# Soft MoE on one Trainium2 core: dispatch weights turned by VectorE, expert products in column halves, loads by use

## The chip, the cores and the metric

The kernel runs on one core of one Trainium2 chip. The metric is the device time of one execution in microseconds (us): 777.72 us in the median of three runs (777.15 to 778.01). About 0.2% is what such runs can tell from no change.

## What is computed

The input x has 8 sequences of 256 tokens and 128 channels. Six sublayers follow each other, each on the layer norm of x: a soft mixture of experts (half weight), linear attention, the same mixture again (half weight), a gated network of five 128/512 layers (half weight), an attention with random features, and the gated network again (half weight). The change is in the mixture. For each sequence:

```python
x = layernorm(x, norm_g, norm_b)                      # (n, d): 256 tokens, 128 channels
se = layernorm(slot_embeds, slot_g, slot_b) * scale   # (e, s, d): 16 experts, 64 slots each
logits = einsum('bnd,esd->bnes', x, se)
dispatch = softmax(logits, axis=1)                    # over the tokens
combine = softmax(logits.reshape(b, n, -1), axis=-1)  # over the 1024 slots
slots = einsum('bnd,bnes->besd', x, dispatch)
gate = gelu(einsum('besd,edf->besf', slots, Wg) + bg)
up = einsum('besd,edf->besf', slots, Wu) + bu         # f: 256
eout = einsum('besf,efo->beso', gate * up, Wd) + bd
out = einsum('bns,bso->bno', combine, eout)
```

All is in fp32.

## The kernel before, in words

**Order of the work.** The kernel is written as steps. A step (class `Step`) names the engines that can do it with a planned cost in ns, what it reads and writes, and the buffers it takes. `Plan.place` (line 122) is a list scheduler: it gives each step an engine, a start and a buffer slot, by earliest start and then by a key. `LAG` (line 73) is the planned delay from one engine's end to another's start. The key follows the PE work planned so far, plus a shift for each part of the program (`SHIFTS`, line 16), numbers that a search has found. `issue` (line 193) emits all instructions in order of planned start; each engine then runs its own list strictly in that order on the chip, and waits on semaphores. DMAs are mostly issued from SP's queue.

**Groups.** The 8 sequences form two groups of four (`group`, line 1286). Group 1's keys are set 45,000 ns behind those of group 0, so that the two groups interleave. Within a group: dispatch of four sequences, 16 experts on the slots of all four, combine and linear attention per sequence; the second mixture; the gated network; the random features; the gated network again, which stores the result.

**Keys** (line 448). The slot embeddings are normalized, turned by TensorE (`flip`, line 355: a transpose against the identity, line 356) and stored as `seT`, with a third copy (line 489) so that odd sequences can read the two halves of a 128-slot block in reversed order.

**Dispatch** (line 523), once per sequence and mixture, 16 times in all. `norm` and `normalized` (line 373) make y: statistics on VectorE, the root on GpSimd (lines 392 and 393), the application on GpSimd or VectorE (line 399). `transposed` (line 419) turns y; `logits` (line 537) has four rounds of two matmuls, copied to `comb` by `evacuated` (line 358; ScalarE line 363 or VectorE line 365), and a running maximum (line 554). Then, for each half of 512 slots: the maximum over tokens (569), exponentials with sums (577), reciprocal (585), division on GpSimd (590). The result `ex` has slots on partitions; the gather needs tokens there. So TensorE turns it in 128-squares (`turn`, line 598: eight flips per half, copied from PSUM to `dm` in two copies of 128x512) and `gathered` (611) makes two fp32 matmuls of 512 columns. `affinely` (436) puts the result, with gain and bias of the norm, into `sl`. At last the maximum over slots is turned (639), reduced, spread over the partitions (651, matmuls against the identity), subtracted on GpSimd (663) and exponentiated (669), for the combine.

**Experts** (line 675). `fetch` (684) loads an expert's matrices and its bias `bd`. `front` (694) makes gate and up (703), GELU (709) and the product (714). `back` (726) makes, for each expert, four matmuls with 128 stationary columns, which are 64 slots of two sequences, and 128 moving columns (733), and adds the bias in two operations of 64 partitions (743). The outputs overwrite the slots of the block in `sl`.

**Buffers** (line 229): `comb` 9 of 8 KB per partition, `k4` 6, `we` 3, eight PSUM banks, and others.

**Loads.** All weights of the other sublayers are loaded at the start (`load`, line 260), the small vectors one by one, from the queues of SP, ScalarE and GpSimd. x is loaded in pairs of sequences (282 and 289), the embeddings in halves from ScalarE's queue (279).

The attention with random features already uses tiles of TensorE's array: `projected` (line 1168) runs four 32-row tiles, `products` (line 1261) four 32-column tiles.

Of the kernel before, what the change touches and what calls it, by code (L numbers as in the profile page):

```python
# [16 lines left out]
    -1227, -613, -401, -68, -58, -18, -64, -450, -1382, -1020, -424, -281, -256, -288, -233,  # L17
    -157, -79, -415, -2474, -2414, -2140, -1616, -1392, -1410, -1361, -1647, -1993, -981, -1024,
    -765, -300, -356, -285, -548, -633, -125, 202, -436, 1069, 1221, 47, 271, -1474, 20, 20,
    328, 135, 321, 41, 324, 244, 344, -354, 285, -285, 130, -858, -387, -2, -20, -1081, -1196,  # L20
    -1025, -690, 2, -62, -155, -432, -31, 11, 73, 364, -325, 423, 704, 1277, 1488, 0, -230,
    -498, -161, 261, 336, -1069, -2039, -294, 15, -985, -97, 217, 334, -2546, -904, 699, 282,
    280, 343, -499, -1613, -348, 575, -245, 854, 1080, -1505, 7, 181, -43, 85, 275, 63, 263,
    275, -549, 207, -31, 105, -21, -515, -1151, -524, -514, -318, -600, -516, -298, -150, -63,
    -195, -1899, -1808, -1825, -1479, -1755, -1468, -2181, -1630, -332, -1392, -135, -1924,
    -2484, -1986, -1337, -312, -863, 129, -9, -422, 292, 66, 420, 268, 35, 18, 226, 263, 558,
    1104, 691, -956, -1572, -901, -704, -964, -1303, -1243, -1820, -2476, -2535, -1146, -830,
    -744, 683, -666, -1356, -722, 275, 396, -1669, -293, -1310, -784, 170, 576, 457, 239, 57,
    785, 684, 309, 781, 1213, 1341, 704, 927, 758, 229, 1188, -1400, 467, 1275, -975, 2, 61,
    -923, 156,  # L30
# [34 lines left out]
class Plan:  # L65
# [7 lines left out]
    LAG = {"PE": 300, "ACT": 120, "DVE": 100, "POOL": 150, "SP": 2200}  # L73
# [128 lines left out]
def macaron_kernel(ctx: ExitStack, tc: tile.TileContext, i: dict, out: bass.AP):  # L202
# [27 lines left out]
        "comb": (NJ * N, 9),  # L230
        "slots": (NJ * NB * 4 * S1, G),
        "k4": (1024, 6),
# [3 lines left out]
        "we": (6 * P + D, 3),  # L236
# [5 lines left out]


    for at, cells in (
        (5000, ["begin"]), (7000, [("x", b) for b in range(B)]), (7500, ["small"]),
        (15000, ["weights"]),
    ):
        plan.given(at, cells)
# [11 lines left out]
    def load(name, shape, src=None, eng=nc.sync):  # L260
        t = const.tile(shape, F32, tag=name, name=name)
        eng.dma_start(t, i[name] if src is None else src)
        return t


    x = const.tile([P, NT, D], F32, tag="x", name="x")
    xin = i["L0_attn_x"].rearrange("b (p t) d -> p b t d", t=TT)
    xout = out.rearrange("b (p t) d -> p b t d", t=TT)

    def x_of(b, n=1):  # L270
        return x[:, b * TT : (b + n) * TT, :].rearrange("p (b t) d -> p b t d", t=TT)

    se_raw = Buf("k4", (P, NJ, D))
    sein = i["slot_embeds"].rearrange("(j p) d -> p j d", p=P)
    for h in range(2):
        part = slice(4 * h, 4 * h + 4)
        step(
            {"SP": 100},
            lambda _, part=part: nc.scalar.dma_start(se_raw.ap[:, part], sein[:, part]),
            ["begin"], [(se_raw, h)],  # L280
        )
    nc.sync.dma_start(x_of(0, 2), xin[:, 0:2])
    sg = load("slot_g", [P, 1], eng=nc.scalar)
    sb = load("slot_b", [P, 1], eng=nc.scalar)
    sc = load("scale", [P, 1], i["scale"].partition_broadcast(P), eng=nc.scalar)
    ng = load("norm_g", [P, 1])
    nb = load("norm_b", [P, 1])
    for q in range(1, 4):
        nc.sync.dma_start(x_of(2 * q, 2), xin[:, 2 * q : 2 * q + 2])
# [60 lines left out]
    def flips(n):  # L350
        return 110 * n
# [164 lines left out]

# [858 lines left out]
```

## Time and profile before

| | us |
|---|---|
| median of three runs | 777.72 |
| the profiled execution | 777.5 |
| its span, first to last instruction | 775.8 |
| busy: PE (matmul) | 754.0 |
| busy: VectorE (DVE) | 528.2 |
| busy: ScalarE (ACT) | 450.4 |
| busy: GpSimd (POOL) | 351.2 |

The page gives for each engine the busy time and the count of instructions, and for groups of instructions their line, tiles, shape, count, busy time and mean duration. An fp32 matmul of the source appears as two instructions, a flip as one. Matmuls are pipelined, so their durations overlap; what one costs is the distance between starts. PEld is the load of stationary operands, beside PE. A window row gives the busy time of each engine in a stretch of the span.

### The profile page before, as it was taken

What the parts mean: (1) busy time and instruction counts of PE and PEld (TensorE: products, weight loads), DVE (VectorE), ACT (ScalarE), POOL (GpSimd) and SP (SyncE); (2) the same over time, 40 slices, a digit from 0 to 9 for tenths busy, and PEclk for the clock granted to TensorE, in tenths of its full rate; (3) what the DMA queues carried; (4) which work ended last, traced back from release to release, by engine and by line L of the source; (5) the groups of instructions that cost most, each with busy time, mean ns of one, the idle gap of its engine ahead of it and who ended that gap; (6) DMA issues with size and microseconds to landing.
All of it is one profiled execution on the core that took longest, in us unless ns stands there. A gap on an engine that the chain in (4) does not pass through costs nothing.

```text
span 775.8 us, 12408 instructions
## 1 busy us (share of the span) xinstructions
PE 754.0 (97%) x4584; PEld 631.6 (81%) x4584; DVE 528.2 (68%) x1156; ACT 450.4 (58%) x824; POOL 351.2 (45%) x376
## 2 busy tenths in 40 slices
PE   2999999999999999999999999999999999999998
PEld 1768787898888988888889879889777887868787
DVE  4899888668988788885645453566865458885422
ACT  1888999555977689987443332345544327543422
POOL 6969454524618356248932123533721326424210
PEclk9999999999999999999999999999999999999999
DMA  7102323203231123232432200000000000000000
GB/s 195 40 0 64 89 65 118 68 29 116 72 114 34 56 68 96 73 86 76 135 95 67 80 1 1 1 1 1 1 1 1 0 15 1 1 1 1 14 0 28
DMA packets 27579, 36.96 MB, mean 48 GB/s; under 512 B 3808, under 2 KB 18816, under 8 KB 27520
## 3 DMA queue, kind: packets, MB, share of 16 engines
q1 hardware_dynamic: 25968, 35.62, 15.6%
q8 instruction: 36, 0.59, 0.3%
q10 hardware_dynamic: 1488, 0.53, 0.3%
q14 instruction: 23, 0.19, 0.1%
q0 software_dynamic: 64, 0.03, 0.0%
HBM read 35.12 MB, written 1.05 MB: 47 GB/s over the span
## 4 chain that ended last, share of the span: by engine, by line
PE 95%; POOL 1%; DVE 1%; DMA 1%; ACT 0%; SPq 0%; issue 0%; POOLq 0%
PE ps L990 25%; PE ps L703 14%; PE ps L772 7%; PE ps L733 7%; PE ps L611 7%; PE ps L537 7%; PE ps L356 6%; PE ps L1090 4%; PE ps L1060 4%; PE ps L1063 4%; PE ps L1230 2%; PE ps L1168 1%; PE ps L1261 1%; PE ps L820 1%; PE ps L651 1%; PE ps L1154 1%
## 5 line engine op out<-in xcount | busy, mean ns | idle before, releaser
L363 ACT COPY k<-ps 128x512 f32<-128x512 f32 (+1 forms) x99 | 51.6, 533 | 128.2 <-PE ps L990 79.7
L703 PE MATMUL ps<-slots,we 128*128 128x256 f32 x512 | 121.0, 380 | 0.0
L703 PEld LDWEIGHTS ps<-slots,we 128*128 128x128 f32 x512 | 93.8, 189 | 16.6 <-issue 4.3
L990 PE MATMUL ps<-comb,comb 128*128 128x256 f32 x448 | 102.8, 380 | 0.0
L990 PE MATMUL ps<-comb,slots 128*128 128x256 f32 x448 | 101.9, 381 | 0.0
L663 POOL TENSOR_TENSOR comb<-comb,k 128x1024 f32<-128x1024 f32 x32 | 75.1, 2365 | 57.3 <-ACT k L577 29.6
L990 PEld LDWEIGHTS ps<-comb,slots 128*128 128x128 f32 x448 | 83.8, 190 | 13.4 <-issue 1.9
L990 PEld LDWEIGHTS ps<-comb,comb 128*128 128x128 f32 x448 | 83.4, 190 | 11.8 <-issue 1.4
L975 POOL TENSOR_TENSOR comb<-comb 128x512 f32<-128x512 f32 x20 | 30.6, 1530 | 123.9 <-ACT comb L1012 73.3
L590 POOL TENSOR_TENSOR k<-k,sm 128x1024 f32<-128x1024 f32 x32 | 60.6, 1903 | 35.7 <-DVE sm L585 34.3
L356 PE MATMUL ps<-ident,k 128*128 128x128 f32 x408 | 60.1, 276 | 15.1 <-POOL k L399 13.6
L714 DVE SCALAR_TENSOR_TENSOR k<-ps,bu,k 128x256 f32<-128x256 f32 x128 | 57.3, 477 | 22.7 <-ACT k L709 21.7
L709 ACT ACTIVATE k<-ps,bg 128x256 f32<-128x256 f32 x128 | 56.4, 473 | 26.1 <-PE ps L703 25.2
L1004 DVE TENSOR_TENSOR comb<-ps,k 128x512 f32<-128x512 f32 x48 | 33.0, 688 | 55.2 <-PE ps L990 31.9
L356 PEld LDWEIGHTS ps<-ident,k 128*128 128x128 f32 x408 | 49.0, 143 | 26.0 <-POOL k L399 14.6
L733 PEld LDWEIGHTS ps<-we,k 128*128 128x128 f32 x512 | 63.9, 192 | 4.9 <-issue 2.4
L743 DVE TENSOR_TENSOR slots<-ps,we 64x256 f32<-64x256 f32 x128 | 53.8, 421 | 20.3 <-PE ps L733 17.4
L537 PE MATMUL ps<-k,seT 128*128 128x256 f32 x256 | 63.4, 389 | 2.5 <-ACT k L441 1.6
L733 PE MATMUL ps<-we,k 128*128 128x128 f32 x512 | 65.4, 275 | 0.0
L577 ACT ACTIVATE k<-comb,sm 128x256 f32<-128x256 f32 x128 | 63.3, 497 | 1.4 <-DVE sm L569 1.2
L1012 ACT ACTIVATE comb<-comb 128x512 f32<-128x512 f32 x48 | 29.9, 628 | 54.2 <-DVE comb L1004 54.1
L772 PE MATMUL ps<-slots,comb 128*128 128x129 f32 x512 | 60.4, 275 | 0.0
(144 smaller groups left out, 1425.5 us busy)
## 6 DMA issues: line engine op xcount, KB each, us to landing
we<-in_We SPq DMA_DIRECT2D x64, 384.0 KB, 3.1
we<-in_bd SPq DMA_DIRECT2D x64, 64.0 KB, 3.1
x<-in_L_attn_x SPq DMA_DIRECT2D x4, 256.0 KB, 5.8
comb<-in_h2T SPq DMA_DIRECT2D x4, 256.0 KB, 3.3
slots<-in_h1T SPq DMA_DIRECT2D x4, 256.0 KB, 4.9
out<-x SPq DMA_DIRECT2D x8, 128.0 KB, 1.7
k<-in_slot_embeds ACTq DMA_DIRECT2D x2, 256.0 KB, 6.2
k<-in_hs SPq DMA_DIRECT2D x2, 256.0 KB, 4.3
```

The lines of the kernel that those rows point to most:

```text
L356: nc.tensor.transpose(po, src, ident)
L537: mm(pl.ap[:, j, :], seT[:, 2 * u + j, odd : odd + 2].rearrange("p k s -> p (k s)"), yt.ap, start=True, stop=True,)
L577: nc.scalar.activation(ex.ap[:, j, :], comb.ap[:, 4 * h + j, :], AF.Exp, bias=mx.ap[:, j : j + 1], accum_out=mx.ap[:, 4 + j : 5 + j],)
L590: nc.gpsimd.tensor_tensor(ex.ap, ex.ap, mx.ap[:, 8:12].unsqueeze(2).to_broadcast([P, 4, N]), ALU.mult)
L611: mm(po.ap.rearrange("p j k s -> p (j k s)"), y.ap[:, t, :], dm.ap[:, t, :], start=(t == 0), stop=(t == TT - 1),)
L663: nc.gpsimd.tensor_tensor(raw, raw, mb.ap.unsqueeze(1).to_broadcast([P, 4, N]), ALU.subtract)
L703: mm(pe.ap[:, m, :], we.ap[:, ts(2 * m + c, P)], sl.ap[:, j, :, k::2, 0:S], start=True, stop=True,)
L709: nc.scalar.activation(ga.ap, pe.ap[:, 0, :], AF.Gelu, bias=bg[:, e, c : c + 1])
L714: nc.vector.scalar_tensor_tensor(ht.ap[:, c, :], pe.ap[:, 1, :], bu[:, e, c : c + 1], ga.ap, ALU.add, ALU.mult,)
L733: mm(po.ap[:, q, :], ht.ap[:, c, ts(q, P)], we.ap[:, ts(4 + c, P)], start=(c == 0), stop=(c == 1),)
L772: mm(po.ap[:, t, 0 : D + 1], comb.ap[:, j, ts(t, P)], eo()[:, j, q, 0 : D + 1], start=(j == 0), stop=(j == NJ - 1),)
L990: mm(bank.ap[:, o], w(k)[:, c, ts(o, P)], rhs().rearrange("p (c n) -> p c n", c=2)[:, c, :], start=(start and o + c == 0), stop=(stop and ...
```

## The change

**Turned on VectorE.** `ex` is now one `comb` buffer for all 1024 slots. VectorE transposes each half in place, in squares of 32 (two instructions of 128x1024 per dispatch). The 16 flips, their four copies to `dm` and `dm` are gone. After such a turn, the partitions 32a to 32a+31 hold 32 tokens, for the slots 32a to 32a+31 of every block. So each of the four groups of 32 rows needs all tokens of y in its own 32 partitions: `replicated` writes y to DRAM (four DMAs) and reads it back four times (four DMAs) into `yr`, all from SP. `gathered` makes 8 x 4 matmuls with 32 rows, each row group into its own PSUM bank, and each bank is put into `sl` by `affinely`, 256 columns at a time.

**Down products.** `back` now handles a pair of experts: the two experts' slots go to the two halves of the partitions, by tiles of 64 columns, and one 128x512 operation adds both biases. `sl` and `seT` change their layout for it, and the third copy in `seT` goes. `back` of a pair follows the `front` of the expert after it.

**Loads.** x, embeddings and one packed `small` come first, from SP in steps that the plan orders: x one sequence at first, the keys in quarters. The other weights (`later`) may be loaded only behind the first copy of y. `keys` works in quarters.

**Other.** `spread` uses flips. The norm's root negates the mean (one GpSimd instruction more) so that the application adds; the addition of 1e-6 on GpSimd becomes a multiplication by 1 and an addition. At the start ScalarE runs one exponential on a constant and TensorE 14 matmuls of the identity by itself (`rehearse`). `comb` has 10 buffers, `k4` 4, `we` 4. SP's planned lag is 2600 ns instead of 2200, some planned costs change, and all shifts are new.

```diff
-            for t in range(TT):
-                pt = ps_(4, P)
...
-                step({"PE": flips(4)}, turn, [ex], [pt], takes=[dm])
-                evacuated(
...
+            def turn(_, part=part):
+                nc.vector.transpose(
+                    ex.ap[:, part].rearrange("p j n -> p (j n)"),
+                    ex.ap[:, part].rearrange("p j n -> p (j n)"),
+                )
+
+            step({"DVE": 1200}, turn, [(ex, h)], [(ex, h)])
+
+        pos = [ps_(NJ, 32) for _ in range(4)]
+
+        def gathered(_):
+            for c in range(N // 32):
+                for a, po in enumerate(pos):
+                    rows = slice(32 * a, 32 * a + 32)
                     mm(
-                        po.ap.rearrange("p j k s -> p (j k s)"), y.ap[:, t, :], dm.ap[:, t, :],
-                        start=(t == 0), stop=(t == TT - 1),
+                        po.ap, yr.ap[rows, c, :], ex.ap[rows, :, 32 * c : 32 * c + 32],
+                        start=(c == 0), stop=(c == N // 32 - 1), tile_position=(32 * a, 0),
                     )
+        step({"PE": 3600}, gathered, [yr, (ex, 0), (ex, 1)], pos)
+
+        for a, po in enumerate(pos):
             affinely(
-                lambda h=h: sl.ap[:, 4 * h : 4 * h + 4, q // 2, blocks, 0:S],
-                lambda po=po: po.ap, [po], [(sl, j, q) for j in range(4 * h, 4 * h + 4)], 512,
+                lambda a=a: sl.ap[:, :, a // 2, q, 32 * (a % 2) : 32 * (a % 2) + 32],
+                lambda po=po: po.ap, [po], [(sl, "in", q, a)], NJ * 32,
             )
```

```diff
+    def replicated(y, b):
+
+        yr = Buf("k4", (P, N // 32, D))
+
+        def spill(_):
+            for k in range(4):
+                nc.sync.dma_start(
+                    spilled[b].rearrange("i (t k) d -> i k t d", k=4)[:, k],
+                    y.ap[32 * k : 32 * k + 32],
+                )
+
+        def spread(_):
+            for a in range(4):
+                nc.sync.dma_start(yr.ap[32 * a : 32 * a + 32], spilled[b])
```

```diff
             def down(_):
-                for q in range(NB):
+                for q in range(BG):
                     for c in range(2):
-                        mm(
-                            po.ap[:, q, :], ht.ap[:, c, ts(q, P)], we.ap[:, ts(4 + c, P)],
-                            start=(c == 0), stop=(c == 1),
-                        )
+                        for k in range(2):
+                            mm(
+                                po.ap[S * k : S * k + S, q, :], hts[k].ap[:, c, ts(q, S)],
+                                wes[k].ap[:, ts(4 + c, P)], start=(c == 0), stop=(c == 1),
+                                tile_position=(0, S * k),
+                            )
...
             def biased(_):
-                for u in range(2):
-                    rows = slice(u * S, (u + 1) * S)
-                    nc.vector.tensor_tensor(
-                        eo()[rows, j, (u ^ k) :: 2, 0:D], po.ap[rows],
-                        we.ap[rows, 6 * P :].unsqueeze(1).to_broadcast([S, NB, D]), ALU.add,
-                    )
+                nc.vector.tensor_tensor(
+                    eo()[:, j, :, 0:D], po.ap,
+                    wes[0].ap[:, 6 * P :].unsqueeze(1).to_broadcast([P, BG, D]), ALU.add,
+                )
```

```diff
         def spread(_):
             for t in range(TT):
-                mm(
-                    pb.ap[:, ts(t, P)], mn.ap[:, t : t + 1].to_broadcast([P, P]), ident,
-                    start=True, stop=True,
-                )
+                flip(pb.ap[:, ts(t, P)], mn.ap[:, t : t + 1].to_broadcast([P, P]))
...
+    plan.key = -100000
+    x_in(0, 1)
+    keys_in(0)
+    fetched(lambda: small, i["small"], [], ["small", "ng"])
+    keys_in(1)
+    x_in(1, 1)
+    keys_in(2)
+    keys_in(3)
...
+    def rehearse(_):
+        for _ in range(14):
+            mm(pwarm.ap, ident, ident, start=True, stop=True)
```

## The prediction

> **What bounds the kernel now.** I read the page first, for the engine shares and the chain that ended last.
>
> ```profile
> PE 754.0 (97%) x4584; PEld 631.6 (81%) x4584; DVE 528.2 (68%) x1156; ACT 450.4 (58%) x824; POOL 351.2 (45%) x376
> ...
> PE 95%; POOL 1%; DVE 1%; DMA 1%; ACT 0%; SPq 0%; issue 0%; POOLq 0%
> ```
>
> TensorE (PE) is busy nearly throughout and 95% of the chain is its own work. Second, the windows by stage (columns: stretch, its length, busy time of PE, PEld, DVE, ACT, POOL, clock, DMA share, GB/s):
>
> ```profile
> 0.00:11.30 11.30, 0.00 (x0) 0.00 (x0) 3.10 (x18) 1.28 (x1) 4.89 (x22) 1.00 0.68 203
> 11.30:22.45 11.15, 6.76 (x21) 4.32 (x21) 7.64 (x34) 3.65 (x6) 10.45 (x17) 1.00 0.71 200
> 22.45:57.70 35.25, 34.66 (x173) 26.13 (x174) 32.05 (x56) 31.07 (x90) 27.49 (x23) 1.00 0.00 1
> 57.70:140.00 82.30, 80.94 (x445) 66.11 (x444) 69.73 (x144) 77.53 (x146) 49.74 (x37) 1.00 0.29 85
> 140.00:500.00 360.00, 359.54 (x2215) 312.39 (x2215) 246.10 (x588) 218.21 (x413) 166.42 (x191) 1.00 0.23 67
> ```
>
> See two regimes. After 140 us PE alone is full. From 22 to 140 us VectorE (DVE) and ScalarE (ACT) are at 85 to 94% beside it: there they are nearly as late as PE. Before 22 us PE waits for data.
>
> A busy PE says little of its pace, so third I read starts in PE's timeline (start us, us, line, shape, count); the step from one row's start to the next, over the count, is the price of one instruction.
>
> ```profile
> 48.69 1.04 PE L356 MATMUL ps<-ident,k 128*128 128x128 f32 x8
> 49.56 3.60 PE L611 MATMUL ps<-k,k 128*128 128x512 f32 x8
> 53.00 1.03 PE L537 MATMUL ps<-k,seT 128*128 128x256 f32 x4
> ...
> 61.90 1.06 PE L651 MATMUL ps<-ident,sm 128*128 128x128 f32 x8
> 62.80 1.05 PE L703 MATMUL ps<-slots,we 128*128 128x256 f32 x4
> 63.68 1.05 PE L733 MATMUL ps<-we,k 128*128 128x128 f32 x8
> 64.57 1.88 PE L611 MATMUL ps<-k,k 128*128 128x512 f32 x4
> ```
>
> A flip (L356) costs 0.87/8 = 0.109 us, L611 3.44/8 = 0.430, L537 0.86/4 = 0.216, L651 0.112, L733 0.89/8 = 0.111. Each fp32 matmul of the source is two such instructions, a flip is one. The same view where the kernel already tiles the array (L1168: 32-row tiles; L1261: 32-column tiles):
>
> ```profile
> 505.35 0.96 PE L1154 MATMUL ps<-half,k 128*128 128x16 f32 x8
> 506.24 1.17 PE L1168 MATMUL ps<-pbd,k 32*128 32x128 f32 x32
> 507.34 1.99 PE L990 MATMUL ps<-comb,slots 128*128 128x256 f32 x8
> ...
> 548.38 1.07 PE L1261 MATMUL ps<-k,kv 128*32 128x256 f32 x16
> 549.38 1.13 PE L1060 MATMUL ps<-k,w1T 128*128 128x512 f32 x2
> ```
>
> 32 row-tiled instructions take 1.10 us: eight groups of four at 0.112 (0.90) and 0.20 more. 16 column-tiled ones take 1.00: four groups of four at 0.216 (0.86) and 0.14 more. So four tiles run side by side, in fp32 too. Around a block another 0.08 goes ahead (L1123's four from 547.85 would be over at 548.30, the block starts at 548.38) and 0.10 behind (the two L990 from 507.34 together last 0.70, not 0.60). I take **0.35 us per tiled block**, from 0.32 to 0.38.
>
> Last, the start:
>
> ```profile
> 16.86 3.78 PE L537 MATMUL ps<-k,seT 128*128 128x256 f32 x8 [0.87 <-ACT seT L477]
> 20.43 0.86 PE L356 MATMUL ps<-ident,k 128*128 128x128 f32 x6
> ```
>
> The first eight logits take 3.57 us from start to start, against 1.73 later: PE runs at half pace though the clock column reads 1.00.
>
> [...]
>
> **The change, part by part, on PE.**
> (1) Dispatch. Gone per call: 16 flips (1.74) and 8 of L611 (3.44), 5.18 us. New: 32 matmuls, 64 instructions, of 32 rows and 256 columns. By L1168's concurrency 16 groups at 0.216 = 3.46, and 0.35 for the block: 3.81. Times 16 calls: **-22.0**. The 32-element runs that the moving operand now has are in no row; if they slow the stream, up to 0.4 a call, +6; if the block's edges vanish, -6.
> (2) `spread`: L651's 64 at 0.112 become 32 flips at 0.109: **-3.7**.
> (3) Down products. A pair of experts has 16 instructions of 0.111 today, 1.78. After: 32 with 64 columns, two side by side, 16 groups at 0.112 = 1.79, so no gain in streaming, and one tiled block: +0.35. 32 pairs: **+11.5** (from +3 if the edges overlap to +19). Two halves of 64 columns are in no row; L1261 is the nearest.
> PE's own work: -22.0 - 3.7 + 11.5 = **-14.2**.
>
> **On the other engines.** DVE and ACT lose, per dispatch, four 128x512 copies (0.59 to 0.68) and two affine evictions (0.8), 4.1 us, and gain two transposes of 128x1024 and four affine evictions of 256 columns (0.55). A transpose is unpriced here: [...] nearest row, L569's reduction of the same size, 1.21[...]. I take 1.2: +0.5 us per dispatch, nothing in sum. The bias add of a pair falls from four of 0.42 (L743) to one of 0.69: 1.0 us of DVE for 32 pairs. After 140 us all this lies under PE and is worth nothing. The POOL edits (one more 0.23 us instruction in each norm; applies and the 1e-6 add in a two-operation form, planned cheaper) lie under PE too; at the start they nearly cancel.
>
> The trip of y through DRAM adds eight DMA issues per dispatch, on SP alone: some 0.43 each, 3.4, and two landings of about 3 (the weights' median is 3.1): 10 us from y to its copy. It lies beside logits, maxima, exps, the division and the turn (about 11 us); uncovered, gather waits for the difference. Behind a waiting spread stand the expert weights on SP. Those loads are planned ahead and SP's waits are long (L688 waits 223 us in all for a free buffer), so I cost it at nothing; if that cover failed, 1 to 3 us per dispatch in the first four. The experts' own issues stay four per pair. Of the buffers, one more `we` and one more `comb` can only loosen; two fewer `k4` hold, since `ex` moves to `comb` and `dm` is gone.
>
> **The start.** The page's DMA share is 0.7 until 22 us, from weights loaded all at once; these move behind the first use, and the many one-column loads become one. In the first 58 us PE holds 72 L537, 84 flips, 24 L611, 8 L651 and 6 L703: 15.6 + 9.2 + 10.3 + 0.9 + 1.3 = 37.3 us of work, so 20.7 are lost. After: x comes alone and first, landing near 3.7 (issue at 0.8, 0.42 for it, 2.5, under the weights' 3.1); two stats 0.9; a quarter of the keys stats 0.9; POOL's roots 1.2 each; apply 0.9; flip, eviction 0.6 and hand-offs: first logits near 10, not 16.86[...]. PE would be steady 9 to 10 us sooner than today's 22.45. But what is late next is DVE and ACT: at 63 busy of 70.5 engine-us they set the pace from there to the first experts, they get no lighter per dispatch, while PE needs 1.8 us less for each of some three dispatches. So about 4.5 of it come back as holes in PE: **-5.0**. Between 58 and 140 the same pressure costs **+1.5**, half a dispatch's saving. The tail (3.8 us) stays.
>
> **Sum.** -14.2 - 5.0 + 1.5 = -17.7, from the profiled execution's own 777.5 (span 775.8, 1.7 around it; median 777.72): **760.0**.
>
> **Rivals.**
> A, the forecast: 754 to 766, chance 0.45.
> B, DVE and ACT as the bound until 140 us, with four PSUM banks held at once by a gather. For it: ACT at 94%; against it: group 1's dispatches can fill holes. Most of the saving of four more dispatches is lost (7 us): 767, to 774. Chance 0.17.
> C, better: holes filled (-6) and tile edges at half (48 x 0.17 = -8): 746, to 754. For it: the order is free to pair blocks; against it: the edges in both blocks shown. 0.26.
> D, slower: the two column halves don't run side by side. Then 32 pairs pay 16 more slots of 0.112: +57, 817. It decides from a pair that takes 0.55 us more than my 2.14. Against it: L1261 overlaps. 0.06.
> E, the new order doesn't fit the chip, PE waits eat the saving: 777. 0.06.
>
> **How the numbers follow.** The likeliest, 760.0. 746 to 772 leaves out D, most of E and the ends of B and C, under 0.2. 0.2% is what a measurement can tell from no change. Faster: A, B, C and a third of E, 0.90; same 0.03; slower, D and a rest, 0.07.
>
> **What would show it.** Right: gather blocks near 3.8 us from start to start, down blocks near 2.1, first logits near 10 us, PE again full after 140, the transpose at 1.1 to 1.3. Wrong: down blocks over 2.7; transposes of 2 us and more; PE waits for DMA of the copy of y; holes in PE beyond 140 us.

## The result and the profile after

The changed kernel takes **770.75 us** in the median of four runs (769.17 to 773.03), against 777.68 us for the kernel before on the same chip: ratio 0.9914, 95% interval 0.9892 to 0.9936. It is faster by 7, not by the forecast 17.7. Over the nine runs of the changed kernel in this document the time goes with the clock that TensorE was granted: 768.1 to 769.2 us where its mean was 0.993, 770.2 to 773.0 us where it was 0.991 or 0.989. The profiled execution took 770.3 us, its span is 768.4, so 7.4 less than the span before.

The page after, the engines' shares and the chain that ended last:

```profile
PE 745.4 (97%) x5732; PEld 631.1 (82%) x5732; DVE 517.7 (67%) x1074; ACT 431.1 (56%) x804; POOL 315.6 (41%) x427
...
PE 92%; DVE 5%; ACT 1%; POOL 1%; issue 1%; DMA 0%; POOLq 0%
```

The chain has gained 4% of VectorE, some 30 us, at the cost of PE. The windows of the changed kernel, columns as in the prediction, say where:

```profile
0.00:11.30 11.30, 7.27 (x38) 6.08 (x39) 6.19 (x33) 3.18 (x5) 7.66 (x32) 1.00 0.70 201
11.30:22.45 11.15, 10.14 (x37) 7.83 (x37) 8.34 (x17) 6.68 (x17) 10.41 (x22) 0.70 0.59 152
22.45:57.70 35.25, 23.36 (x194) 18.38 (x192) 34.01 (x52) 27.59 (x79) 28.08 (x17) 0.85 0.44 123
57.70:140.00 82.30, 81.71 (x852) 70.59 (x849) 67.19 (x128) 64.35 (x135) 40.66 (x40) 1.00 0.33 99
140.00:500.00 360.00, 357.89 (x2928) 310.32 (x2930) 233.67 (x526) 198.39 (x395) 162.01 (x217) 1.00 0.25 77
```

PE starts sooner, as forecast. Then, from 22 to 58 us, where it was busy 34.66 of 35.25 us, it is busy 23.36, and VectorE 34.01. After 58 us PE is full again. The clock column, 1.00 all through before, reads 0.70 and 0.85 in the second and third row: TensorE was granted half its clock from 11.3 to 18.1 us and again from 42.0 to 52.2 us.

For a sum by stretch I price every PE instruction of the trace at its steady step (0.216 us for 256 columns, 0.109 for a flip, 0.112 for 128, tiled ones divided by the tiles side by side; the rehearsal not counted as work) and take that work from the length of the stretch. What remains is lost time:

| stretch, us | lost before | lost after |
|---|---|---|
| 0 to 22.4 | 19.2 | 14.0 |
| 22.4 to 58 | 1.6 | 16.5 |
| 58 to 140 | 2.0 | 4.6 |
| 140 to 500 | 1.3 | 13.2 |
| from 500 | 9.3 | 9.0 |
| all | 33.4 | 57.3 |
| PE's work at its steps | 742.4 | 711.1 |

The work falls by 31.3 us, the lost time grows by 23.9. Of the latter 14.5 lie between 58 and 500 us: the edges of the tiled blocks, which the forecast had. The other 9.7 lie in the first 58 us, where it had -5.0. PE's timeline of the changed kernel shows the place (in brackets: idle time before, and whom it waited for):

```profile
10.38 2.86 PE L565 MATMUL ps<-k,seT 128*128 128x256 f32 x8
...
38.13 0.43 PE L357 MATMUL ps<-ident,sm 128*128 128x128 f32 x2 [0.60 <-DVE sm L669]
45.36 0.47 PE L357 MATMUL ps<-ident,k 128*128 128x128 f32 x1 [6.80 <-DVE k L402]
...
48.86 5.35 PE L565 MATMUL ps<-k,seT 128*128 128x256 f32 x16 [0.73 <-DVE k L446]
...
67.24 3.72 PE L565 MATMUL ps<-k,seT 128*128 128x256 f32 x16
```

The first logits start at 10.38 us. At 38 us a hole of 6.8 us opens ahead of the turn of group 1's first sequence. The last row, 16 logits, starts as soon as the fourth gather is over. I use it as a **mark**: the first four dispatches are done. The fourth gather before, the row of L611 at 64.57 us in the prediction, ended at 66.4. So the dispatches end when they ended, though PE began 6.5 us sooner and has less to do in each. (By then the old kernel had also done 24 instructions of the first experts, 4.4 us at their steps, but seven instructions of logits fewer, so it was some 3 us further.)

What VectorE did in the hole, and what GpSimd did beside it, in the same trace:

```profile
40.56 6.97 POOL L687 TENSOR_TENSOR comb<-comb,k 128x1024 f32<-128x1024 f32 x3
42.98 4.63 DVE L402 TENSOR_SCALAR k<-x,sm 128x128 f32<-128x128 f32 x2
```

Two applications of the norm take 4.63 us on VectorE; elsewhere one takes 0.33. GpSimd runs three subtractions of 128x1024 (`less`, for the combine) at the time, 2.32 us each, and each application ends with one of them. The chain view of the same trace goes from there to TensorE:

```profile
43.06 4.55 DVE k L402 x2
...
48.86 5.35 PE ps L565 x16
```

From 19 us to 48.7 us this chain is VectorE's; from 48.86 us on it is TensorE's own work up to the mark, with 0.56 us of ScalarE in it. Its first piece, the 16 logits, runs at half clock until 52.2 us:

```profile
42.00:52.20 10.20, 4.28 (x10) 3.10 (x11) 9.37 (x13) 5.79 (x13) 10.10 (x6) 0.50 0.07 16
```

16 logits at full clock take 3.72 us (the row of 67.24), so 1.6 us of the chain lie in the clock.

### The profile page after: what moved, and what is told of

It reads as the page before. It is cut to its first block, busy times and chain, and to the rows that moved or that the text cites. A ratio compares the mean times of both kernels' runs of the same rounds, so it can differ in the third digit from the quotient of the medians.

```text
span 768.4 us, 14822 instructions
## 1 busy us (share of the span) xinstructions
PE 745.4 (97%) x5732; PEld 631.1 (82%) x5732; DVE 517.7 (67%) x1074; ACT 431.1 (56%) x804; POOL 315.6 (41%) x427
## 4 chain that ended last, share of the span: by engine, by line
PE 92%; DVE 5%; ACT 1%; POOL 1%; issue 1%; DMA 0%; POOLq 0%
PE ps L1024 25%; PE ps L734 14%; PE ps L765 8%; PE ps L806 8%; PE ps L641 7%; PE ps L565 6%; PE ps L1124 4%; PE ps L1094 4%; PE ps L1097 3%; PE ps L357 3%; PE ps L1266 2%; PE ps L1297 1%; PE ps L1202 1%; PE ps L854 1%; DVE k L402 1%; DVE sm L599 1%
## 5 line engine op out<-in xcount | busy, mean ns | idle before, releaser
L364 ACT COPY k<-ps 128x512 f32<-128x512 f32 (+1 forms) x68 | 33.6, 498 | 108.8 <-PE ps L1024 78.6
L620 POOL TENSOR_TENSOR comb<-comb,sm 128x1024 f32<-128x1024 f32 x32 | 60.9, 1909 | 55.6 <-DVE sm L615 55.4
L740 ACT ACTIVATE k<-ps,small 128x256 f32<-128x256 f32 x128 | 56.6, 475 | 40.6 <-PE ps L734 39.6
L745 DVE SCALAR_TENSOR_TENSOR k<-ps,small,k 128x256 f32<-128x256 f32 x128 | 56.8, 476 | 27.7 <-ACT k L740 27.3
L607 ACT ACTIVATE comb<-comb,sm 128x256 f32<-128x256 f32 x128 | 63.3, 497 | 2.5 <-DVE sm L599 2.3
L765 PE MATMUL ps<-we,k 128*64 128x128 f32 x1024 | 62.1, 275 | 0.0
L765 PEld LDWEIGHTS ps<-we,k 128*64 128x64 f32 x1024 | 55.3, 137 | 7.6 <-issue 3.8
L641 PE MATMUL ps<-comb,k 32*128 32x256 f32 x1024 | 61.1, 381 | 0.2 <-DVE slots L777 0.2
L806 PEld LDWEIGHTS ps<-slots,comb 128*128 128x128 f32 x512 | 59.1, 192 | 1.9 <-issue 1.3
L394 POOL TENSOR_SCALAR sm<-sm 128x2 f32<-128x2 f32 x52 | 10.0, 193 | 123.2 <-DVE sm L388 121.4
```

The lines of the kernel that those rows point to most:

```text
L364: nc.scalar.copy(dst(), src())
L607: nc.scalar.activation(ex.ap[:, 4 * h + j, :], comb.ap[:, 4 * h + j, :], AF.Exp, bias=mx.ap[:, j : j + 1], accum_out=mx.ap[:, 4 + j : 5 + j],)
L620: nc.gpsimd.tensor_tensor(ex.ap[:, part], ex.ap[:, part], mx.ap[:, 8:12].unsqueeze(2).to_broadcast([P, 4, N]), ALU.mult,)
L641: mm(po.ap, yr.ap[rows, c, :], ex.ap[rows, :, 32 * c : 32 * c + 32], start=(c == 0), stop=(c == N // 32 - 1), tile_position=(32 * a, 0),)
L740: nc.scalar.activation(ga.ap, pe.ap[:, 0, :], AF.Gelu, bias=bg[:, e, c : c + 1])
L745: nc.vector.scalar_tensor_tensor(ht.ap[:, c, :], pe.ap[:, 1, :], bu[:, e, c : c + 1], ga.ap, ALU.add, ALU.mult,)
```

## Experiments

Two theories stood at first. **Stall:** GpSimd's two-input operations hold up VectorE, and VectorE's chain sets the end of the first four dispatches. **Work:** VectorE simply has more to do, the transposes above all. Later a third came up, that the hole itself and PE's slow rate behind it are the loss.

**The changed kernel again**, beside the next four.

> The changed kernel once more, as the measure for the runs beside it: both theories 769 to 773 us.

Measured: 770.16 us (768.08 to 771.53), ratio 0.9902 (0.9887 to 0.9916). In its profile (768.08 us) the mark is at 65.05 us. From the mark on it takes 703.0 us, as the first profile of the changed kernel does (770.3 - 67.24 = 703.1). In that first profile PE ran slower before 22 us: the eight logits of 10.38 us took 2.86 us there, 1.95 here, where the granted clock was 1.00 until 39.4 us. So the 2.2 us between the two marks go with the early half clock. The chain view of this second profile is like the first, but from 51 to 56 us, between logits and third gather, it runs through ScalarE's and VectorE's work for the fourth dispatch.

**No subtraction in the first four dispatches.** In these, the maximum over slots is left out of the combine weights:

```diff
+                if early:
+                    return
                 raw = comb.ap[:, 4 * h : 4 * h + 4, :]
                 nc.gpsimd.tensor_tensor(
...
+                    nc.scalar.activation(raw, raw, AF.Exp, bias=fixed)
```

(`fixed` holds -75.)

> In the first four dispatches (group 0, first mixture) the subtraction of the token's maximum on GpSimd is left out; the exponential takes a constant of -75 in its place, which divides out. The planned order stays. Theory 1 (the start is bound by VectorE, which GpSimd's two-input operations stall on top, so that PE's saved work turns into waiting): the 2.3 us applications and the 7 us hole in PE at 38 us shrink, 4 to 8 us less than the changed kernel, 763 to 767. Theory 2 (the edges of the 48 tiled blocks ate the gain): no change, within 1.5 us.

Measured: 765.33 us, ratio 0.9846 (0.9827 to 0.9864), 4.8 under the changed kernel; the mark at 61.14. The groups of VectorE up to 67 us in this kernel have

```profile
L404 DVE TENSOR_SCALAR k<-x,sm 128x128 f32<-128x128 f32 x4 | 1.3, 343 | 0.2 <-POOL sm L398 0.2
```

so four applications take 343 ns each. In the changed kernel the same four take 1.35 us each. The run takes GpSimd's work away together with the stall, so it doesn't tell the two apart.

**A one-input operation in its place.** GpSimd adds -75 by `tensor_scalar`; the maximum is left out in the same way.

```diff
+                if early:
+                    nc.gpsimd.tensor_scalar(raw, raw, -75.0, None, ALU.add)
+                    return
```

> The same four dispatches subtract the constant 75 on GpSimd with a one-input operation in place of the two-input one with the token's maximum. It is longer (2.8 us for such a size in the kernel before, not 2.4). Theory 1[...]: VectorE's applications fall from 2.3 to 0.35 us and the time falls by 2 to 5 us, 766 to 769. If it is only GpSimd's own time that is late: 1 to 3 us more, 772 to 774. Theory 2: no change.

Measured: 767.63 us, ratio 0.9871 (0.9858 to 0.9884), 2.5 under the changed kernel; the mark at 63.94. The groups up to 67 us:

```profile
L689 POOL TENSOR_SCALAR comb<-comb 128x1024 f32<-128x1024 f32 x8 | 22.4, 2817 | 0.3
...
L402 DVE TENSOR_SCALAR k<-x,sm 128x128 f32<-128x128 f32 x4 | 1.3, 379 | 0.6 <-POOL sm L396 0.6
```

GpSimd works longer than before (2.82 us each, not 2.41) and VectorE's applications are short. But as a test of the stall this is weak: the two applications were issued at 41.58 and 41.83 us, when the operation beside them had 0.41 and 0.15 us left, and the first ended 0.08 us behind it (0.48 us). The kernel before has a better case, two applications beside a one-input addition of 128x1024:

```profile
551.10 2.78 POOL L1200 TENSOR_SCALAR comb<-comb 128x1024 f32<-128x1024 f32 x1
...
552.14 0.59 DVE L399 TENSOR_SCALAR k<-x,sm 128x128 f32<-128x128 f32 x2
```

Both are over more than 1 us before GpSimd is, at 0.34 us each: no hold. The gain is only half of what taking the subtraction away gives. In the chain view of this run GpSimd's subtractions and divisions stand from 39.2 to 51.3 us, so GpSimd's own time counts too.

**No turn on VectorE.** In the first four dispatches `turn` does nothing, so that the gather takes unturned weights.

```diff
             def turn(_, part=part):
+                if early:
+                    return
                 nc.vector.transpose(
```

> The first four dispatches leave out VectorE's transposes (eight of 1.23 us), so their gather adds up the wrong products. Order as planned. Theory 1: VectorE is the bound until 67 us, 5 to 9 us less than the changed kernel, 762 to 766. Theory 2: no change, within 1.5 us.

Measured: 769.66 us, ratio 0.99 (0.9883 to 0.9917): 0.5 under the changed kernel, not 5 to 9. Ten us of VectorE's work are gone and the time stays. That the turns decide falls here; VectorE's other work was not taken away. Two turns do stand on the chain of the changed kernel, just ahead of the applications. In this trace ScalarE's exponentials stand there in their place, and the applications behind them still take 4.67 us.

**Both left out**, the subtraction and the turn.

> In the first four dispatches both GpSimd's subtraction (a constant in the exponential stands for it) and VectorE's transposes are left out; the gather there adds up wrong products. Each alone gave -4.8 and -0.5. If GpSimd's two-input operations hold VectorE until they end, so that work removed from VectorE alone is waited out anyway, both together give more than the sum: 7 to 9 us less than the changed kernel, 761 to 763. If VectorE's transposes are not on the path at all: the same as without the subtraction, 765.

Measured: 766.3 us, ratio 0.985 (0.9831 to 0.9869), mark at 60.84: as without the subtraction alone. The chain views of the two runs tell why. Without the subtraction alone, a turn is among the last pieces ahead of the applications; with both left out, it is ScalarE's exponentials, to 38.66 us:

```profile
38.18 1.13 DVE comb L631
...
36.68 1.98 ACT comb L610 x8
```

The applications start at 40.39 us in the one and at 40.29 us in the other. Two chains are equally late here, so taking work from one of them gains nothing.

**Down products whole.** Four instructions with 128 columns again; the outputs land in another order of slots.

```diff
-                for q in range(BG):
-                    for c in range(2):
-                        for k in range(2):
+                for k in range(2):
+                    for q in range(2):
+                        for c in range(2):
...
-                                po.ap[S * k : S * k + S, q, :], hts[k].ap[:, c, ts(q, S)],
+                                po.ap[:, 2 * k + q, :], hts[k].ap[:, c, ts(q, P)],
...
-                                tile_position=(0, S * k),
```

> The down products of a pair are made untiled, with 128 stationary columns as before the change, 16 instructions in place of 32; the rows then stand at the wrong places, so the experts' outputs are permuted. Same order. The trace of the changed kernel has a tiled down block at 1.90 us from start to start, 0.09 ahead and 0.10 behind it: 2.09, untiled 1.79. If the edges cost just that (theory 1), 32 x 0.30 = 9.6 us less than the changed kernel's 770.2, 760 to 762. If tiling costs more than the starts show, or the columns slow other work (theory 2), 14 us less or more, 756 or under.

Measured: 765.99 us, ratio 0.9842 (0.9827 to 0.9856), 4.2 under the changed kernel, not 9.6. From the mark on it takes 698.8 us, so 4.2 less than 703.0: the column halves cost 4.2 us net, all behind the mark. That is 5.4 us less than expected. Part of it the traces show: in the changed kernel the 32 pairs stand in 28 stretches of down products, eight of whose ends touch a gather, so taking the tiles away removes 48 changes of tiling and not 64, 1.5 us at 0.095 each; and 1.2 us come back as waits for expert matrices (`we<-in_We`). The other 2.7 us are not accounted for.

**Filler behind the third spread.** 28 products of the identity with itself in the hole, to see whether the 16 logits behind it then come at PE's pace of 3.72 us.

> 28 idle matmuls of the identity (56 instructions, 6.3 us of PE) are added in the hole of PE at 38.5 us, after the third dispatch's spread. If PE's work in the start is worth nothing and only its clock counts: no longer, and 1.5 to 2.5 us less, since the 16 logits behind the hole take 3.5 instead of 5.4 us: 768 to 769. If PE still counts there: up to 6 us more, 773 to 776.

Measured: 774.84 us, ratio 0.9961 (0.9946 to 0.9976), 4.7 slower. A bad place: the filler shares the bank of `spread`, so its eviction and all of `less` behind it came later. It doesn't tell what it should.

**One rehearsal product instead of 14.**

> One matmul in place of the 14 of the rehearsal at the start. The first logits are on the path; they took 2.9 us for eight with the rehearsal, 3.6 in the kernel before without it. 0.7 to 2 us more than the changed kernel, 771 to 772; if the start of PE counts for nothing, no change.

Measured: 770.72 us, ratio 0.9909 (0.9895 to 0.9923): no difference in the medians to be told. The profiles do differ: the first eight logits took 3.78 us here and 1.95 in the second profile of the changed kernel, and the mark is at 67.07 against 65.05. But in the first profile, with the rehearsal and the half clock from 11.3 to 18.1 us, they took 2.86 us and the mark is at 67.24.

**Filler ahead of a turn.** The same 28 products ahead of the flips of a norm, meant for group 1's first.

```diff
+            if fill:
+                for _ in range(28):
+                    mm(
+                        pt.home["ps"][pt.slot][:, 256:384], ident, ident,
+                        start=True, stop=True,
+                    )
             for t in range(n):
                 flip(pt.ap[:, t, :], y.ap[:, t, :])
```

> Adds 28 products of the identity with itself (128x128) on TensorE ahead of the first turn of the first sequence of group 1, in the hole of 7 us, into columns of the bank that nobody reads; nothing waits for them but the turn itself, which waits for VectorE until 45.4 us anyway. Theory C (what the hole costs is also the slow rate of TensorE behind it: 16 logits in 5.35 us, against 3.5 at its pace): the logits come back to 3.5 to 4.2 us, 1 to 2 us gained, 768.5 to 770. Rival (VectorE's chain decides until 67 us, so the rate of TensorE there is of no account): within 0.7 us of the changed kernel, 770 to 771.

Measured: 777.73 us, ratio 0.999 (0.9982 to 0.9999), 7.6 slower than the changed kernel. My count of the turns was wrong: the filler ran at 185 us, where PE has no gap. So it prices work on PE there: 6.5 us busy cost 7.6 us, in full. Then the same in the hole, with the condition on the part of the plan instead of a count:

> The 28 products of the identity with itself, this time where they were meant: on TensorE ahead of the first turn of the first sequence of group 1, in its hole of 7 us (they went to 185 us in the run before, where they cost 7.5 us in full). Theory C (TensorE is slow for the 16 logits behind the hole because it stood idle): the logits take 3.5 to 4 us in place of 5.1 to 5.4, 1 to 2 us gained, 768.5 to 769.5. Rival (VectorE's chain decides until 65 us): within 0.7 us of the changed kernel, 769.7 to 771.

Measured: 770.48 us, ratio 0.9907 (0.9891 to 0.9924): no change. PE's timeline in this kernel:

```profile
36.57 6.52 PE L432 MATMUL ps<-ident 128*128 128x128 f32 x56
...
46.83 5.13 PE L574 MATMUL ps<-k,seT 128*128 128x256 f32 x16 [0.81 <-DVE k L454]
...
65.03 3.72 PE L574 MATMUL ps<-k,seT 128*128 128x256 f32 x16
```

6.5 us more of work in the hole cost nothing, and the mark stays at 65.03. PE has that time to spare. The rate of the logits wasn't tested: after two more waits (2.0 and 0.8 us) they are still slow, 5.13 us. The granted clock stayed at 1.00 until 46.3 us here, but it was 0.50 from there to 49.7 us, and in the second profile of the changed kernel it is 0.50 until 49.6. So the half clock over the hole itself costs nothing; what it costs over the logits stays open.

**The norm of group 1 earlier**, so that PE has its logits for the hole. Only the order of the steps changes.

```diff
+        early = {"stats": 16900, "root": 18000, "apply": 19500, "run": 38250}
+        for s in self.placed:
+            name = s.run.__name__
+            if s.part == 102 and name in early and s.start < 44000:
+                s.start = early[name]
```

> Nothing is left out; only the place of four steps in the order of the engines changes: the normalization of the first sequence of group 1 (stats, root, apply, and the turns that go with it) is issued where VectorE and GpSimd have their first gap (its statistics near 17 us instead of near 37 us of the order's own time), so that it is done before GpSimd's two subtractions of two inputs at 42.9 and 45.2 us. Theory H (the 7 us hole of TensorE at 38 to 45 us is a matter of the order: nothing is ready there but this sequence, whose normalization stands behind the dispatch on VectorE and is stretched there by GpSimd): the turns follow the last spread without the hole, the wait of L357 on VectorE falls from 6.8 to under 2 us, some 5 to 8 us come back, 762 to 765. Rival (the dispatch chain on VectorE up to the fourth gather sets the end, and the hole is only slack on that chain): the hole is filled early but opens again before the fourth gather near 67 us, under 1.5 us gained, 769 to 771.

Measured: 770.32 us, ratio 0.9902 (0.9883 to 0.992), as the changed kernel. This run needs a caution: I had moved the eviction of the turned values ahead of the turns, so the logits of that sequence are of other values. The same caution holds for the next, which leaves out the subtraction besides:

> The earlier normalization and, for the first four dispatches, no subtraction of the maximum on GpSimd (the exponential takes a constant of -75 in place of the sequence's own maximum; this leaves out the maximum from the computation of those four). Theory H with the stall of VectorE under GpSimd's two-input operation as a separate cost: the two add up in part, since the earlier normalization avoids the two stretched applications but not the stretched folds: 760 to 763, 2 to 3 us under the earlier normalization alone. Rival (both remove the same stall): the same as the earlier normalization alone, within 1 us.

Measured: 769.6 us, ratio 0.9895 (0.9879 to 0.9911). It lost the 4.8 us that leaving out the subtraction had given: the first gather starts at 36.87 us, against 30.91 without the subtraction alone. With the turns ahead of their eviction:

> Nothing is left out. The earlier normalization once more; in the run before, the eviction of the turned values was issued ahead of the turns themselves and so read the bank too soon; now the turns come first. Theory P (the chain of VectorE and GpSimd through the first four dispatches sets the end, and the hole of TensorE is slack on it): the logits of group 1 move ahead of 45 us, the fourth gather ends where it did (65 to 66 us), 769 to 771. Rival H (the hole itself is the loss): 763 to 766.

Measured: 771.03 us, ratio 0.991 (0.9896 to 0.9924): no gain. PE's timeline in it:

```profile
25.10 0.43 PE L363 MATMUL ps<-ident,sm 128*128 128x128 f32 x2 [2.86 <-DVE sm L675]
...
35.88 3.87 PE L647 MATMUL ps<-comb,k 32*128 32x256 f32 x64
...
43.67 5.26 PE L571 MATMUL ps<-k,seT 128*128 128x256 f32 x16 [2.15 <-ACT comb L613]
51.97 3.74 PE L647 MATMUL ps<-comb,k 32*128 32x256 f32 x64 [3.04 <-DVE comb L634]
...
65.25 3.72 PE L571 MATMUL ps<-k,seT 128*128 128x256 f32 x16
```

The hole of 6.8 us is gone, and its time has moved: 2.86 us at 25, where VectorE now does the norm (its two applications take 2.16 us there; in the trace of the first of these three runs they take the same 2.16 us, beside a division of 1.89 us on GpSimd, so the stall has moved along), and 3.04 us at 52, ahead of the second gather. The mark is at 65.25. But the first gather, at 35.88 us, starts 4.6 us later than in the second profile of the changed kernel (31.26), and from there to the mark this run is 4.4 us shorter. So it filled the hole and paid for it ahead of it, and doesn't tell what the hole alone costs. With the free filler it says this much: TensorE's own work there is not the limit, and when the hole ends is set by the other engines.

**The two applications on GpSimd**, ahead of its subtractions, so that they can't be held up.

```diff
+        root = [s for s in self.placed if s.part == 102 and s.run.__name__ == "root"][0]
+        for s in self.placed:
+            if s.part == 102 and s.run.__name__ == "apply":
+                s.engine, s.start = "POOL", root.start
```

> Nothing is left out. The two applications of the normalization of the first sequence of group 1, which VectorE does at 41 to 45.5 us of the changed kernel in 2.3 us each, go to GpSimd, right behind their root and ahead of its two subtractions of two inputs. Theory L (VectorE is held up in these two by GpSimd's two-input operation, and VectorE's chain sets the end of the first four dispatches): two applications cost GpSimd 0.9 us, VectorE loses 4.6 us of work and stall, the turns come near 40 us, the fourth gather ends 3 to 4 us sooner (near 62 us, as without the subtraction), 766 to 767.5. Rival M (the removed subtraction helped because GpSimd itself, busy 10.4 of 10.6 us there, sets the pace): 0.9 us more on GpSimd, so no gain or a loss, 770 to 771.5.

Measured: **768.22 us**, ratio 0.9879 (0.9865 to 0.9892), 1.9 under the changed kernel, mark at 62.91. A gain in the median, though GpSimd has more to do; this is the run that speaks for the stall and against GpSimd's amount of work as the whole cause. It is less than expected and not far out of the noise: the intervals of the two ratios touch, the runs overlap (767.2 to 769.3, and 768.1 to 771.5), and of the 2.1 us by which the mark is sooner the profiled run lost 1.9 again behind it. VectorE has the 4.6 us free and then waits for GpSimd, as the chain view shows:

```profile
39.57 6.95 POOL comb L691 x3
46.52 3.71 POOL comb L624 x2
```

The divisions that the next gathers need (the second row) stand behind the three subtractions, until 46.5 us.

**Divisions ahead of subtractions** on GpSimd, on top of that.

```diff
+        late = {165: 39400, 122: 41000, 177: 41100, 166: 42300, 123: 42400,
+                178: 44600, 179: 56000, 136: 56100, 180: 58000, 137: 58100}
+        for s in self.placed:
+            s.start = late.get(s.number, s.start)
```

(165 and 122 are divisions, 166 and 123 turns, 177, 179 and 136 subtractions, 178, 180 and 137 their exponentials.)

> Nothing is left out. As with the applications on GpSimd, and besides, GpSimd does the four divisions that the second to fourth gathers wait for ahead of three subtractions that nobody needs before the experts are through (with the two turns and three exponentials that go with them moved to match). Theory P (GpSimd's and VectorE's chain ahead of the gathers decides): the divisions no longer stand behind 7 us of subtractions, the gathers start near 48, 51.5 and 55.5 us, the logits behind the fourth near 59.5 in place of 62.9, so 3 to 4 us under the applications on GpSimd alone: 764 to 765.5. Rival Q (ScalarE's exponentials, ready near 45 and 47.5 us, decide): the last gather can't start before 57 us, under 1.5 us gained, 767 to 768.5.

Measured: 774.32 us, ratio 0.9962 (0.9948 to 0.9976), 6.1 slower than without it. In PE's timeline:

```profile
45.71 5.77 PE L573 MATMUL ps<-k,seT 128*128 128x256 f32 x16 [5.66 <-DVE k L454]
```

The two turns stood on VectorE ahead of the eviction that group 1's logits need, and ScalarE's last exponentials stand behind the copies of these logits. Three queues in strict order: moving steps on one alone moved the wait. So the other two had to follow:

```diff
+        late = {165: 39400, 198: 40740, 122: 40800, 205: 41000, 1214: 42200,
+                1215: 42300, 1218: 42310, 201: 42330, 206: 42340, 196: 43085,
+                202: 43090, 166: 43100, 1219: 43145,
...
+                209: 43160, 177: 43170, 179: 43180, 136: 43190,
+                178: 51200, 180: 58100, 137: 59500}
```

> Nothing is left out. The run before put the four divisions ahead of three subtractions on GpSimd alone and lost 6 us, since other queues still held the last two back: VectorE took two turns ahead of the eviction that group 1's logits wait for (5.7 us of TensorE), and ScalarE's last exponentials stood behind the evictions of those logits (51 us). Now ScalarE's and VectorE's orders follow: the last sequence's maximum and both its exponentials directly behind each other, the eviction ahead of the turns, the subtractions' exponentials behind the evictions of the gathers. Theory P (GpSimd's, VectorE's and ScalarE's chain ahead of the gathers decides the first 65 us): divisions at 39.5 to 47.5 us, turns to 49, gathers from 48 on one behind the other, the logits behind the fourth near 59.5 in place of 62.9: 764 to 765.5. Rival Q (what bounds is these engines' amount of work, in whatever order): 767 to 769.

Measured: **766.98 us** (764.61 to 768.89), ratio 0.9863 (0.9845 to 0.9881). The mark:

```profile
61.54 3.72 PE L577 MATMUL ps<-k,seT 128*128 128x256 f32 x16
```

That is 3.5 us sooner than in the second profile of the changed kernel (65.05), and the median is 3.2 lower than its 770.16. Both orders are the chain's own: the same instructions, placed otherwise. In the two profiles the times are 2.2 us apart (765.85 and 768.08), so 1.3 of the 3.5 were lost behind the mark. The expectation was 59.5, so the rest, 2 us, isn't reached. Its chain is VectorE's until 52.8 us, with a maximum of 1.46 us (L670, elsewhere 0.42) beside two of GpSimd's subtractions, and TensorE's from there; that wasn't tried. This version beats the kernel before and the changed one.

**All marks together.** In the profile of each kernel, the profiled time less the mark is 703.0 to 705.0 us for the changed kernel and all of these but two: whole down products (698.8) and the filler at 185 us (710.1). So what these edits moved on GpSimd, VectorE and ScalarE acted ahead of the mark, to within 2 us, and behind it PE's own work decides.

## Why the prediction was wrong, point by point

**PE's own work, -14.2: right, a little better.** The streaming saved is 31.3 us in the trace, 31.2 in the prediction (16 x (5.18 - 3.46) + 3.7). The edges were to take 17.1 of it and took about 14.5, all waits between 58 and 500 us counted as edges. A gather block takes 3.67 us from start to start, with 0.09 ahead and 0.10 behind 3.86 (forecast 3.81); a down block 1.90, with edges 2.09 (forecast 2.14). The page and the timeline after:

```profile
L765 PE MATMUL ps<-we,k 128*64 128x128 f32 x1024 | 62.1, 275 | 0.0
...
214.75 1.97 PE L765 MATMUL ps<-we,k 128*64 128x128 f32 x32
216.65 0.71 PE L641 MATMUL ps<-comb,k 32*128 32x256 f32 x6
```

32 instructions start within 1.90 us, 59 ns apart, so two column halves do run side by side, and rival D is out. The third row shows a gather directly behind, over one shared edge. **The size that was off:** +11.5 for the down halves, which took their edges as never shared; the run without them gained 4.2. That the sum is near is in part luck: 7.3 too much here stands against about 5 too little for all other losses between 58 and 500 us (14.5 - 4.2 = 10.3, forecast 17.1 - 11.5 = 5.6). Which these are wasn't tried.

**The start, -5.0: the step that failed.** Its first half was right: first logits at 10.38 us (forecast near 10), and 5.2 us less lost by 22.4 us. Its second half said that VectorE and ScalarE set the pace from there, that "they get no lighter per dispatch", and that "about 4.5 of it come back as holes". That the other engines decide was right, the size was not: 15 us came back between 22 and 58, and not only the earlier start but everything that PE saves in the first four dispatches. Three things were missed in it.
- I added up VectorE's and ScalarE's busy time as one pool of 63 of 70.5 us. What holds is a chain: VectorE's from 19 to 48.7 us in the first profile, with ScalarE's exponentials as late beside it and GpSimd's subtractions and divisions next. GpSimd was left out (its edits were to "lie under PE too"). Its divisions and subtractions are 36.2 us of the first 67 in the second profile of the changed kernel (17 operations of 1.9 and 2.4 us).
- VectorE is held up by these operations: two applications, elsewhere 0.33 us each, took 4.63, and each ended with one of GpSimd's two-input subtractions. The prediction had no term for it. Beside GpSimd's one-input addition of 128x1024 there was no hold: in the kernel before, two of VectorE's applications took 0.34 us each in the midst of one.
- Up to the logits behind the hole a saving on PE is no saving, since others decide when they start: PE's filler of 6.5 us in the hole cost nothing. What the first four dispatches save there should have been left out of the -22.0, unless the chain gets shorter as well.

How far this is shown: the best edit (no subtraction) gave 4.8 us back, the best order 3.2. About 2 us of the 9.7 are the half clock before 18 us (marks 67.24 and 65.05) and up to 1.6 the half clock behind the hole; no edit removed either. That the rest is VectorE's and ScalarE's own work in this order is argued from the chain and from VectorE's 34.0 of 35.3 us; no run shows it.

In numbers: 9.7 in place of -5.0 is 14.7 worse; the edges are 2.6 better, and the 1.5 for 58 to 140 us was not needed, since that stretch holds no more than its edges; 0.3 less is lost at the end. 17.7 - 14.7 + 2.6 + 1.5 + 0.3 = 7.4, the difference of the spans.

**The transpose at 1.2 us: right.** It takes 1.23 us for 128x1024 (1.20 to 1.25 for all 32 of the trace). Leaving it out in four dispatches changed nothing, since ScalarE is as late.

**y by way of DRAM, at nothing: right.** No gather waited for the copy in the trace; the 0.2 us of its waits end with a bias add (L777). **After 140 us** PE waits for next to nothing but its edges, as forecast.

**Rivals.** The result lies in B's band (767 to 774): other engines are the bound early, and the saving of the early dispatches is lost. B's place was wrong, 58 to 140 us and VectorE with ScalarE; it is ahead of 65 us, with GpSimd. E, an order that doesn't fit the chip, has a part in it: two edits of the order gave 3.2 us back.

## What to carry to other kernels

Where a stage has several engines near 90%, follow the chain through them from one end to the other, GpSimd too, before counting a saving on TensorE there; a saving counts from the point where TensorE itself is late. Idle work put into a hole of TensorE tells what TensorE's own work there is worth: if it costs nothing, a saving on TensorE ahead of the hole gains nothing. It doesn't tell what an earlier end of the hole would gain; for that, speed up what releases it. And look at the granted clock over a hole before pricing the work behind it (here 0.50 for 10.2 us). In a kernel with queues in strict order, a step that is moved must take the steps that feed and follow it on the other queues along, or the wait moves too (774.3 against 767.0 us here).

## What the runs showed of the hardware

- Beside GpSimd's `tensor_tensor` of 128x1024, instructions of VectorE from SBUF to SBUF were held up in the first profile of the changed kernel: two `tensor_scalar` of 128x128 at 42.98 us, each until a subtraction ended (2.3 us instead of 0.33), and a `tensor_tensor` of 128x256 at 27.15 us beside a division of 1.89 us that began at 27.02 (2.04 us instead of 0.42). VectorE's transposes beside the subtractions took their usual 1.2 us (1.23 at 24.24 us, 1.21 at 40.62). GpSimd's one-input addition of 128x1024 did not hold the `tensor_scalar` (0.34 us twice, at 552 us of the kernel before).
- GpSimd's one-input addition of 128x1024 took 2.82 us in the run with it, the two-input subtraction of the same size 2.41 in the second profile of the changed kernel. With a multiplication and an addition in one `tensor_scalar` of that size (L1234 of the changed kernel), it took 1.05.
- In a hole of 6.8 us (38.56 to 45.36 us of the first profile) and behind it TensorE was granted half its clock for 10.2 us (42.0 to 52.2 us), and the 16 logits of 256 columns behind the hole took 5.35 us; in the other runs shown here, 5.1 to 5.8. At the mark, where the granted clock was 1.00, 16 took 3.72. In the run with the filler in the hole, waits of 2.0 and 0.8 us stood directly behind 6.5 us of full work, and the granted clock was 0.50 for 3.4 us (46.3 to 49.7 us).
